# An LSTM's input products: 16 steps of them moved from the head of the sequence to its tail

## The chip, the cores and the metric

The kernel runs on one core of a Trainium2 chip. The metric is the device time of one execution in microseconds (us); three timed runs stand for the kernel before. One further execution was taken by the hardware profiler, and every trace row below is from it.

## The reference

An LSTM over 512 steps with a batch of 32 and 512 hidden units, whose outputs are added to its input. Everything is float32.

```python
xW = einsum('ntd,dg->ntg', x, Wx) + b        # (32, 512, 2048)
def step(carry, xw_t):
    prev_h, prev_c = carry
    a = xw_t + prev_h @ Wh
    i, f, o = (sigmoid(a[:, k*512:(k+1)*512]) for k in range(3))
    g = tanh(a[:, 3*512:])
    next_c = f * prev_c + i * g
    next_h = o * tanh(next_c)
    return (next_h, next_c), next_h
out = x + hs                                  # hs: next_h of all steps
```

`prev_h @ Wh` can only be made step by step (the recurrence). `x @ Wx` (the x products) can be made at any time before its step.

## The kernel before

**The recurrence.** `h_part(t)` multiplies the transposed h by `wh_sb` into two PSUM banks of `gates`: first the columns of i, f and g (384 a quarter), then those of o (128). `cell(t)` follows: sigmoid and tanh on ScalarE (ACT), products and sums on VectorE (DVE), and a transpose `ht` on DVE that releases the next `h_part`. `seed_first` and `seed_last` (ACT) copy the x product of a coming step into its `gates` bank before its recurrence adds to it.

**Three ways to x products.** Steps are grouped in rows of eight (`ROW`).
- *Plain* (`direct`): 16 matmuls of 512 columns a step, straight from the row and `Wx` (`raw`), in four quarters; `keep_direct` adds the bias on DVE. Before the change only steps 0 to 7.
- *Head units* (rows 1 to `HEAD`/8 - 1; four units a row): a fast scheme with seven products in place of eight for two by two blocks of the row and of Wx. It needs differences of Wx (`t_sums`, three DVE instructions for each of the eight pieces of Wx) and of the row (`inner_sums`).
- *Superblocks* of 24 steps (`PER`, three rows): a scheme on top of that with 20 jobs of seven products each (`A_OPS`, `B_OF`, `C_OPS`). Its 14 factors that mix several pieces of Wx are made once by DVE in the head (`make_factors`), written to DRAM (`keep`) and read again for each superblock (`fetch`, into the rings `wa` and `wb`).

Head units and superblocks are drained from PSUM by `evacuate` (ACT and DVE) over five windows; results go by the SP queue to DRAM (`store`), return by `load_xw`, and GpSimd (POOL) adds the bias (`add_bias`).

**The order.** It is written out by hand in windows. Step k has one window, k + 4; steps 0 to 2 have two each (`windows_of`). In a window, after `h_part(k)` is issued, come `evacuate`, DVE's due work (`run_due`), the products of up to five jobs (`products`), `fetch`, `cell(k)` and the seeds. All engines take their instructions in this order. `run_due(v, room)` lets due work in by a price of columns + 160 per instruction up to `room` (`ROOM` = 3400), earlier than due if there is room. Factors are due between window 2 and `START`, the window of the first superblock job, 23 steps (`LEAD`) ahead of its use. The last superblock's jobs therefore end about 20 steps before step 511; those last steps have no x products.

**Start.** `load_raw(q)` loads a quarter of Wx by four transfers of 256 KB. Ten matmuls on zeros run first. Then come the plain products of steps 0 to 3 quarter by quarter, of steps 4 to 7 step by step, then the seeds and the first unit.

Of the kernel before, what the change touches and what calls it, by code (L numbers as in the profile page):

```python
# [9 lines left out]
F32 = mybir.dt.float32  # L10
# [4 lines left out]
P = 128  # L15
B = 32
T = 512
NJ = 4
G = 4
IFG = 3 * P  # L20
ROW = 8
NROWS = T // ROW
C = 256
# [11 lines left out]
R = len(A_OF)  # L35

PER = ROW * MO
HEAD = 7 * ROW
DIRECT = ROW
NSB = (T - HEAD) // PER  # L40
assert HEAD + NSB * PER == T

LEAD = 23
NODES = 8
FIXED = 160
ROOM = 3400
SLACK = [1, 1, 3]
AHEAD = 3
UNITS = [(i, j) for i in range(1, HEAD // ROW) for j in range(NJ)]
# [9 lines left out]
START = windows_of(HEAD - LEAD)[0]  # L59
# [4 lines left out]
def begin(n):  # L64

    return 6 * (n // 5) + n % 5
# [7 lines left out]
def kernel(  # L74
# [9 lines left out]
    nc = tc.nc  # L84
# [19 lines left out]
    bias_sb = const.tile([P, G * P], F32, name="bias_sb")  # L104
    h_init = const.tile([P, NJ, B], F32, name="h_init")
    wh_sb = const.tile([P, NJ, NJ, 2 * C], F32, name="wh_sb")
    raw = [const.tile([P, 4, C], F32, name=f"raw_{i}") for i in range(8)]
    tt_ = [const.tile([P, 4, C], F32, name=f"t_{i}") for i in range(8)]
    single = {b[0][0] for b in B_OF if len(b) == 1}

    rows, xw, stored = {}, {}, {}

    def load_row(i, a=0, b=ROW):
        if i not in rows:
            rows[i] = xpool.tile([P, ROW, NJ, B], F32, name=f"row_{i}", tag="row")
        nc.sync.dma_start(
            out=rows[i][:, a:b].rearrange("p t q b -> p (t q b)"),
            in_=x[i][:, a * P : b * P],
        )
# [10 lines left out]

    def load_raw(q):
        k, e = divmod(q, 2)
        for j in range(NJ):
            nc.sync.dma_start(
                out=raw[NJ * k + j][:, 2 * e : 2 * e + 2].rearrange("p n c -> p (n c)"),
                in_=wx[NJ * k + j][:, 2 * e * C : (2 * e + 2) * C],
            )

    nc.scalar.dma_start(out=bias_t, in_=bias)
    c_init = work.tile([P, P], F32, name="c_init", tag="c", bufs=2)  # L140
# [14 lines left out]
    def t_sums(i):  # L155
        w, t = raw[i], tt_[i]
        return [
            lambda: nc.vector.tensor_sub(t[:, 0:2], w[:, 1::2], w[:, 0:2]),
            lambda: nc.vector.tensor_sub(t[:, 2], w[:, 3], t[:, 0]),
            lambda: nc.vector.tensor_sub(t[:, 3], w[:, 2], t[:, 2]),  # L160
        ]
# [54 lines left out]
    def push_factors():  # L216
        done = []
        ops = [op for n in range(R) if len(B_OF[n]) > 1 for op in make_factors(n)]
        for i, (columns, fn) in enumerate(ops):

            def go(fn=fn):
                fn()
                done.append(fn)

            push(2 + (START - 6) * i // len(ops), columns, go, lambda _, i=i: len(done) == i)
# [28 lines left out]
    def run_due(v, room):  # L254

        i = 0
        while i < len(due):
            window, _, columns, fn, ready = due[i]
            if window > v and (columns + FIXED > room or not ready(v)):
                i += 1  # L260
                continue
            assert ready(window)
            due.pop(i)
            fn()
            room -= columns + FIXED
            i = 0
# [109 lines left out]
    def products(v):  # L376
        for late, ss in ((1, (6,)), (4, (4,)), (2, (7,)), (0, (1,)), (0, (5,)), (1, (5,)), (3, (2, 3))):
            job = jobs.get(v - late)
            for s in ss if job else ():
                if s != 5 or job.w5 == v:  # L380
                    product(job, s)
                if s == 4:
                    job.release()
# [163 lines left out]
    def flat(bank):  # L547
        return bank if len(bank.shape) == 2 else bank.rearrange("p n c -> p (n c)")

    def direct(t, bank, qs=range(4)):  # L550
        i, a = divmod(t, ROW)
        for q in qs:
            k, e = divmod(q, 2)
            for j in range(NJ):
                nc.tensor.matmul(  # L555
                    flat(bank)[j * B : (j + 1) * B],
                    rows[i][:, a, q],
                    raw[NJ * k + j][:, 2 * e : 2 * e + 2].rearrange("p n c -> p (n c)"),
                    start=q == 0,
                    stop=True,  # L560
                    skip_group_check=True,
                )

    def keep_direct(t, bank):
        if t < 4:
            xw[t] = upool.tile([P, G * P], F32, name=f"xw_{t}", tag="xw", bufs=4)
        else:
            xw[t] = node_free[t - 4].rearrange("p t e b -> p (t e b)")
        nc.vector.tensor_add(xw[t], flat(bank), bias_sb)  # L569

    def load_xw(t):
        xw[t] = upool.tile([P, G * P], F32, name=f"xw_{t}", tag="xw", bufs=4)
# [81 lines left out]
    def prepare(v):  # L654

        job = jobs.get(v)
        ops = []
        if job is None or job.w >= START:
            return ops
        i, j = job.kind  # L660
        for k in range(2):
            if (i, k) not in head_sums:
                s, more = inner_sums(block(raw_block(i, k)), f"h{i}{k}")
                head_sums[i, k] = s
                ops += more
            if i == 1:
                ops += t_sums(NJ * k + j)
        job.factors = lambda s: [
            (left(block(raw_block(i, k)), s, head_sums[i, k]), raw_factor(NJ * k + j, s)) for k in range(2)
        ]  # L670
        job.finish = finish_unit(job, i, j)
        job.release = lambda: None
        return ops
# [18 lines left out]
    def fetch(v):  # L692

        job = jobs.get(v + 2)
        if job and job.w >= START and len(B_OF[job.kind[1]]) > 1:
            job.ring = [rpool.tile([P, 3, C], F32, name=f"wa_{job.w}", tag="wa", bufs=3), None]
            nc.sync.dma_start(out=job.ring[0].rearrange("p n c -> p (n c)"), in_=kept[job.kind[1]][0])
        job = jobs.get(v)
        if job and job.w >= START and len(B_OF[job.kind[1]]) > 1:
            job.ring[1] = rpool.tile([P, 4, C], F32, name=f"wb_{job.w}", tag="wb", bufs=4)  # L700
            nc.sync.dma_start(out=job.ring[1].rearrange("p n c -> p (n c)"), in_=kept[job.kind[1]][1])
        sb, rest = divmod(v + 6 - START, PER)
        if v + 6 in UNIT_AT[2 * NJ :: NJ]:
            load_row(3 + UNIT_AT[2 * NJ :: NJ].index(v + 6))
        if rest < MO and 0 <= sb < NSB:
            load_row(HEAD // ROW + MO * sb + (0, 2, 1)[rest])

    with tc.manual_schedule():
        warm = work.tile([P, G, P], F32, name="warm", tag="s")
        nc.scalar.activation(warm[:, 0], c_init, AF.Sigmoid)  # L710
        for m in range(10):
            nc.tensor.matmul(  # L712
                pps[0][0:B].rearrange("p n c -> p (n c)"),
                c_init[:, 0:B],
                c_init.unsqueeze(1).to_broadcast([P, 4, P]),
                start=True,
                stop=True,
            )
        nc.vector.transpose(
            bias_sb.rearrange("p (m l) -> p m l", l=B),  # L720
            bias_t.unsqueeze(2).to_broadcast([P, G * NJ, B]),
        )
        firsts = [gates[0], gates[1], pps[0], pps[1]]
        for q in range(4):
            for t in range(4):
                direct(t, firsts[t], (q,))
        for t in range(4):
            keep_direct(t, firsts[t])
        for t, bank in zip(range(4, ROW), (pps[2], accs[0], accs[1], p5)):
            direct(t, bank)  # L730
            keep_direct(t, bank)
        seed_first(0)
        seed_last(0)
        seed_first(1)
        push_factors()
        for op in prepare(0):
            op()
        products(0)
        for op in prepare(1):
            op()  # L740

        for k in range(T):
            if k % 2 == 0 and k + 2 < T:
                load_residual(k + 2)
            if 2 * 4 - 3 <= k and k + 3 < T:
                load_xw(k + 3)
            h_part(k)
            if 2 * 4 - 2 <= k and k + 2 < T:
                add_bias(k + 2)
            for m, v in enumerate(windows_of(k)):  # L750
                if v == START:
                    assert len(due) == 0 or due[0][0] >= START
                    free.extend(t.rearrange("p (h n) c -> p h (n c)", h=2) for t in others)
                announce(v)
                taken = evacuate(v)
                run_due(v, ROOM - taken)
                products(v)
                fetch(v)
                if k == T - 2:
                    x_last()  # L760
                if m == 0:
                    cell(k)
                    seed_first(k + 2)
                    seed_last(k + 1)
                for op in prepare(v + 1):
                    op()
        assert not due
# [51 lines left out]
```

## Time and profile before

| | |
|---|---|
| median of three runs | 3182.22 us (3182.06 to 3183.36) |
| profiled execution | 3179.14 us |
| its span, first to last instruction | 3177.3 us |
| TensorE (PE) busy | 3120.9 us, 98% |
| VectorE (DVE) busy | 2209.9 us, 70% |
| ScalarE (ACT) busy | 1626.0 us, 51% |
| GpSimd (POOL) busy | 937.8 us, 30% |
| moved by DMA | 639.04 MB, mean 201 GB/s |

PE is TensorE's matmuls, PEld its weight loads. Each float32 matmul appears as two instructions; matmuls into four different 32-row strips of a bank overlap, so spacing tells more than the length of one. In a timeline the square brackets hold the idle time of the engine before the row and what ended it. `p` in the rows is the bank p5, `s_h` a head row's sums, `t` the differences of Wx.

### The profile page before, as it was taken

Reading aid. Unit: us, or ns where it says so; the run is one execution under the profiler, and the core shown is the slowest. Engines: PE = TensorE matmul, PEld = TensorE weight load, DVE = VectorE, ACT = ScalarE, POOL = GpSimd, SP = SyncE. Lnnn points to the kernel's source line nnn. Section 1 sums busy time; section 2 is a strip of 40 time slices with the busy share of each in tenths; the row PEclk is TensorE's granted clock in tenths of the full one; section 3 lists DMA queues with packets and bytes.
Section 4 is the critical chain, followed back from the end, with each engine's and each line's share of the span. In section 5 each row is a group of like instructions: output and inputs, shape, how many; then the busy total and the mean of one; then the engine's idle time right before and its main releaser. Section 6 shows DMA issues by size and latency. Waiting matters only on the chain.

```text
span 3177.3 us, 134411 instructions
## 1 busy us (share of the span) xinstructions
PE 3120.9 (98%) x57012; PEld 2035.9 (64%) x57012; DVE 2209.9 (70%) x6155; ACT 1626.0 (51%) x4890; POOL 937.8 (30%) x1017
## 2 busy tenths in 40 slices
PE   8999999999999999999999999999999999999986
PEld 3666666666666666666666676666766666666653
DVE  4573676767777776767777777767777777767652
ACT  1444555555555555555555555555555555555543
POOL 0122232323232332323232332323232333323232
PEclk9999999999999999999999999999999999999999
DMA  4555576756667666757666576757667576667541
GB/s 170 167 164 159 181 232 195 233 187 224 215 198 228 194 224 203 234 177 235 207 206 229 183 231 207 228 189 242 185 218 224 188 231 199 224 209 230 182 152 61
DMA packets 320857, 639.04 MB, mean 201 GB/s; under 512 B 42880, under 2 KB 108672, under 8 KB 319744
## 3 DMA queue, kind: packets, MB, share of 16 engines
q1 hardware_dynamic: 320112, 630.43, 61.7%
q8 instruction: 449, 7.36, 1.0%
q14 instruction: 152, 1.25, 0.1%
q10 hardware_dynamic: 144, 0.01, 0.0%
HBM read 451.75 MB, written 178.52 MB: 198 GB/s over the span
## 4 chain that ended last, share of the span: by engine, by line
PE 91%; DVE 5%; ACT 2%; DMA 1%; issue 1%; SPq 0%; DVEq 0%
PE gates L596 52%; PE acc L367 16%; PE pp L367 16%; PE p L367 5%; DMA xw<-slot 1%; ACT ig L625 0%; DVE c L624 0%; DVE fc L626 0%; DVE fc L622 0%; DVE ht L631 0%; DVE node L302 0%; ACT pp L406 0%; SPq L424 0%; PE pp L712 0%; PE pp L555 0%
## 5 line engine op out<-in xcount | busy, mean ns | idle before, releaser
L596 PE MATMUL gates<-wh_sb,ht 128*32 128x384 f32 x32704 | 1874.3, 379 | 38.8 <-DVE ht L631 35.5
L596 PEld LDWEIGHTS gates<-wh_sb,ht 128*32 128x32 f32 x32704 | 1131.4, 110 | 794.2 <-issue 659.0
L635 POOL TENSOR_TENSOR oc<-xr,ht 128x128 f32<-128x128 f32 x509 | 300.0, 589 | 2144.5 <-DVE ht L631 2115.3
L577 POOL TENSOR_TENSOR xw<-xw,bias_sb 128x512 f32<-128x512 f32 x504 | 656.1, 1302 | 78.1 <-DMA xw<-slot 35.5
L619 ACT ACTIVATE s<-gates 128x256 f32<-128x256 f32 x512 | 196.8, 384 | 777.7 <-PE gates L596 777.6
L408 DVE TENSOR_TENSOR pp<-acc,p 128x256 f32<-128x256 f32 x404 | 174.6, 432 | 275.5 <-ACT pp L407 261.6
L622 DVE TENSOR_TENSOR fc<-s,c 128x128 f32<-128x128 f32 x511 | 150.1, 294 | 203.9 <-ACT s L619 200.3
L626 DVE TENSOR_TENSOR fc<-s,ig 128x128 f32<-128x128 f32 x512 | 149.6, 292 | 192.7 <-ACT ig L625 192.7
L406 ACT COPY pp<-pu 128x512 f32<-128x512 f32 x404 | 242.1, 599 | 49.0 <-DVE slot L514 18.9
L583 ACT COPY gates<-xw 128x384 f32<-128x384 f32 x508 | 240.3, 473 | 20.9 <-DVE xw L569 20.7
L367 PE MATMUL pp<-wb,node 128*32 128x256 f32 x3040 | 246.1, 379 | 0.0
L621 ACT ACTIVATE s<-gates 128x128 f32<-128x128 f32 x512 | 142.0, 277 | 189.0 <-PE gates L596 188.8
L625 ACT ACTIVATE ig<-c 128x128 f32<-128x128 f32 x512 | 158.7, 310 | 139.1 <-DVE c L624 113.7
L407 ACT COPY pp<-acc 128x256 f32<-128x256 f32 x404 | 145.2, 359 | 139.6 <-DVE slot L514 67.0
L631 DVE STREAM_TRANSPOSE ht<-fc 128x128 f32<-128x128 f32 x511 | 159.1, 311 | 54.6 <-DVE fc L626 0.9
L402 DVE TENSOR_TENSOR pu<-acc,p 128x256 f32<-128x256 f32 x404 | 165.7, 410 | 28.1 <-ACT p L399 27.7
L395 ACT COPY pu<-acc 128x256 f32<-128x256 f32 x404 | 150.3, 372 | 58.5 <-PE acc L367 51.3
L367 PE MATMUL acc<-wb,s 128*32 128x256 f32 x2128 | 172.3, 379 | 0.0
L367 PE MATMUL p<-wa,s 128*32 128x256 f32 x2128 | 172.2, 379 | 0.0
L367 PE MATMUL pp<-wb,s 128*32 128x256 f32 x2128 | 172.1, 379 | 0.0
L367 PE MATMUL acc<-wa,s 128*32 128x256 f32 x2128 | 172.0, 379 | 0.0
L399 ACT COPY p<-p 128x256 f32<-128x256 f32 x404 | 152.7, 378 | 31.0 <-PE p L367 24.6
(130 smaller groups left out, 4049.5 us busy)
## 6 DMA issues: line engine op xcount, KB each, us to landing
wb<-keep_b SPq DMA_DIRECT2D x266, 512.0 KB, 5.6
xw<-xw SPq DMA_DIRECT2D x504, 256.0 KB, 4.1
wa<-keep_a SPq DMA_DIRECT2D x266, 384.0 KB, 4.9
xw<-slot SPq DMA_DIRECT2D x656, 128.0 KB, 3.2
xr<-in_x_dram SPq DMA_DIRECT2D x256, 128.0 KB, 3.1
out_dram<-oc SPq DMA_DIRECT2D x255, 128.0 KB, 2.1
row<-in_x_dram SPq DMA_DIRECT2D x63, 512.0 KB, 6.5
xw<-raw SPq DMA_DIRECT2D x252, 128.0 KB, 3.4
```

Of the source, the lines that this page charges most:

```text
L367: nc.tensor.matmul(dst[t * B : (t + 1) * B], a[:, t], w, start=s in (1, 5) and m == 0, stop=True, skip_group_check=True,)
L399: nc.scalar.copy(job.p5, p5[:, 0])
L402: nc.vector.tensor_add(job.pu[:, 1], job.acc, job.p5)
L406: nc.scalar.copy(job.pp[0], job.pu)
L408: nc.vector.tensor_add(job.pp[1][:, 1], job.acc, job.p5)
L577: nc.gpsimd.tensor_add(xw[t], xw[t], bias_sb)
L583: nc.scalar.copy(gates[t % 2][:, 0:IFG], xw[t][:, 0:IFG])
L596: nc.tensor.matmul(g[j * B : (j + 1) * B, cols], state["ht"][:, k, :], wh_sb[:, k, j, cols], start=False, stop=True, skip_group_check=True,)
L619: nc.scalar.activation(s[:, 0:2], g[:, 0:2], AF.Sigmoid)
L625: nc.scalar.activation(tc_t, c, AF.Tanh)
L631: nc.vector.transpose(ht.rearrange("p q b -> p (q b)"), h)
L635: (nc.gpsimd if t < T - 3 else nc.vector).tensor_add(state["oc"][:, tt % 2], xr[t][:, tt % 2], ht)
```

## The change

- `HEAD` is 40, not 56: the head units make rows 1 to 4 instead of 1 to 6, 16 units instead of 24. `START` is the window of step 17, not 33. There are still 19 superblocks.
- `TAIL`: steps 496 to 511 get plain products. From window `FIRST_TAIL`, the first behind the last evacuation (step 477), every window issues two quarters (`tail_products`), behind `products` and so behind that step's recurrence; the next window adds the bias on DVE (`keep_direct`) and leaves the result in SBUF, so these steps need no `load_xw` and no `add_bias`.
- Two pieces of Wx whose room the superblocks use for sums, and the two last rows, are loaded five windows before.
- `t_sums` of all eight pieces, the row sums of unit 0 and the first factors stand on DVE before and between the bias additions of steps 0 to 7; a new `HEAD_ROOM` of 5000 holds in the head.
- Wx comes in four transfers of 1 MB; six matmuls on zeros, not ten.

```diff
-HEAD = 7 * ROW
-NSB = (T - HEAD) // PER
+HEAD = 5 * ROW
+TAIL = 2 * ROW
+NSB = (T - HEAD - TAIL) // PER
+END = HEAD + NSB * PER
+HEAD_ROOM = 5000
...
-    raw = [const.tile([P, 4, C], F32, name=f"raw_{i}") for i in range(8)]
+    raw_sb = const.tile([P, 8, 4, C], F32, name="raw_sb")
+    raw = [raw_sb[:, i] for i in range(8)]
...
-        for j in range(NJ):
-            nc.sync.dma_start(
-                out=raw[NJ * k + j][:, 2 * e : 2 * e + 2].rearrange("p n c -> p (n c)"),
-                in_=wx[NJ * k + j][:, 2 * e * C : (2 * e + 2) * C],
-            )
+        nc.sync.dma_start(
+            out=raw_sb[:, NJ * k : NJ * k + NJ, 2 * e : 2 * e + 2].rearrange("p j n c -> p j (n c)"),
+            in_=wx[NJ * k : NJ * k + NJ, :, 2 * e * C : (2 * e + 2) * C].rearrange("j p c -> p j c"),
+        )
...
+    FIRST_TAIL = START + PER * (NSB - 1) + begin(R - 1) + 6
+    pieces = [(t, q) for t in range(END, T) for q in range(NJ)]
+    tail_rooms, whole = [], []
+    def tail_bank(t):
+        return (*pps, *accs, p5)[t % 6]
+    def tail_products(v):
...
+        for t in whole:
+            keep_direct(t, tail_bank(t), tail_rooms[t - END])
+        whole.clear()
+        for t, q in pieces[:2]:
+            direct(t, tail_bank(t), (q,))
+            if q == NJ - 1:
+                whole.append(t)
+        del pieces[:2]
...
-            if i == 1:
-                ops += t_sums(NJ * k + j)
...
+        if v == FIRST_TAIL - 5:
+            for i in range(8):
+                if i not in single:
+                    raw[i] = rpool.tile([P, 4, C], F32, name=f"raw_again_{i}", tag="wb", bufs=4)
+                    nc.sync.dma_start(out=raw[i].rearrange("p n c -> p (n c)"), in_=wx[i])
+            for i in range(END // ROW, T // ROW):
+                load_row(i)
...
-        for m in range(10):
+        for m in range(6):
...
+        for i in range(8):
+            for op in t_sums(i):
+                op()
+        for op in prepare(0):
+            op()
+        push_factors()
         for t in range(4):
             keep_direct(t, firsts[t])
         for t, bank in zip(range(4, ROW), (pps[2], accs[0], accs[1], p5)):
             direct(t, bank)
+            run_due(0, 2800)
             keep_direct(t, bank)
         seed_first(0)
         seed_last(0)
         seed_first(1)
-        push_factors()
-        for op in prepare(0):
-            op()
         products(0)
...
-            if 2 * 4 - 3 <= k and k + 3 < T:
+            if 2 * 4 - 3 <= k and k + 3 < END:
                 load_xw(k + 3)
...
-            if 2 * 4 - 2 <= k and k + 2 < T:
+            if 2 * 4 - 2 <= k and k + 2 < END:
                 add_bias(k + 2)
...
-                run_due(v, ROOM - taken)
+                run_due(v, (ROOM if v >= START - 4 else HEAD_ROOM) - taken)
                 products(v)
+                tail_products(v)
```

More of the change, by code (lines that the diff above doesn't have):

```diff
@@ L37 @@
 PER = ROW * MO
-HEAD = 7 * ROW
-DIRECT = ROW
-NSB = (T - HEAD) // PER
-assert HEAD + NSB * PER == T
+HEAD = 5 * ROW
+TAIL = 2 * ROW
+NSB = (T - HEAD - TAIL) // PER
+END = HEAD + NSB * PER
+assert END + TAIL == T
 LEAD = 23
@@ L562, in direct, with keep_direct @@
                 )
-    def keep_direct(t, bank):
-        if t < 4:
+    def keep_direct(t, bank, room=None):
+        if room is not None:
+            xw[t] = room
+        elif t < 4:
             xw[t] = upool.tile([P, G * P], F32, name=f"xw_{t}", tag="xw", bufs=4)
@@ L569, in keep_direct @@
         nc.vector.tensor_add(xw[t], flat(bank), bias_sb)
+    FIRST_TAIL = START + PER * (NSB - 1) + begin(R - 1) + 6
[4 more added lines that the diff above has]
+    def tail_products(v):
+        if v == FIRST_TAIL:
+            tail_rooms.extend(node.rearrange("p t e b -> p (t e b)") for node in node_free)
+            for f in free[: (TAIL - len(tail_rooms) + 1) // 2]:
+                tail_rooms.extend([f[:, 0], f[:, 1]])
+            assert len(tail_rooms) >= TAIL
+        if v < FIRST_TAIL:
+            return
+        for t in whole:
[6 more added lines that the diff above has]
+        del pieces[:2]
     def load_xw(t):
```

## The prediction

> **What bounds the kernel now.** I read the page first, then the chain of waits, then the timeline of TensorE at both ends.
>
> ```profile
> span 3177.3 us, 134411 instructions
> ...
> PE 91%; DVE 5%; ACT 2%; DMA 1%; issue 1%; SPq 0%; DVEq 0%
> ```
>
> TensorE carries 91% of the chain, so time goes away only where TensorE has less to do or stands still less. The profiled execution took 3179.14 us (its span and 1.84 us around it); the three timed runs have a median of 3182.22 us, 3.1 us more. I make the sum against the profiled one and take it off the median. About 0.2% (6 us) is the least change a measurement of this kernel can tell.
>
> The prices come from the chain in order of time (start, length, what, instructions):
>
> ```profile
> 11.45 1.29 PE gates L555 x12
> 12.78 0.39 PE gates L555
> 13.16 1.29 PE pp L555 x12
> ...
> 139.74 3.45 PE gates L596 x64
> 143.19 0.86 PE acc L367 x16
> ```
>
> Sixteen instructions of a plain product (512 columns) are spaced 13.16 - 11.45 = 1.71 us. One recurrence, L596, takes 3.45 us. One of the seven products of a head unit, or two of a superblock product's seven, takes 0.86 us.
>
> ```profile
> 44.19 3.64 PE L596 MATMUL gates<-wh_sb,h_init 128*32 128x384 f32 x64
> ...
> 55.72 1.94 PE L367 MATMUL acc<-t,s_h 128*32 128x256 f32 x16 [2.11 <-DVE pu L402]
> ...
> 71.23 1.07 PE L367 MATMUL acc<-t,s_h 128*32 128x256 f32 x16 [2.50 <-DVE pp L408]
> ...
> 309.08 3.66 PE L596 MATMUL gates<-wh_sb,ht 128*32 128x384 f32 x64
> ...
> 3078.90 3.66 PE L596 MATMUL gates<-wh_sb,ht 128*32 128x384 f32 x64 [1.65 <-DVE ht L631]
> 3084.24 3.66 PE L596 MATMUL gates<-wh_sb,ht 128*32 128x384 f32 x64 [1.68 <-DVE ht L631]
> ```
>
> In TensorE's timeline 44.19 is the recurrence of step 0 and 309.08, counted on, that of step 33, whose window is START. In the last steps nothing is left but the recurrence: one every 5.34 us, bound by the loop through ACT and DVE. Of these TensorE issues for 3.45 us, so 1.89 us are free in each. That is the room the change fills.
>
> **The tail.** NSB stays 19 and START moves from step 33 to step 17, so everything from START to the last superblock product keeps its pattern and comes 16 steps earlier. Behind it stand 16 more bare steps: 16 x 5.34 = +85.4 us. In 32 of them two quarters of a plain product (16 instructions, 1.71 us) stand behind the recurrence in TensorE's queue. 3.45 + 1.71 = 5.16 us, under 5.34: they are hidden by 0.18 us, with nothing but the cell's loop as cover. Without cover they would cost 32 x 1.71 = 55 us. I take 0 and keep +3 us (0.1 us too many in each) for the range; below 0 there is nothing to win, the loop being unchanged. The bias additions run on DVE before the cell needs it, while it waits for the recurrence.
>
> At the seam the SP queue gets four loads of 512 KB (two pieces of Wx, two rows), the Wx pieces waiting for TensorE to let go of a ring buffer. The next load of xw stands behind them.
>
> ```profile
> xw<-xw SPq DMA_DIRECT2D x504, 256.0 KB, 4.1
> ```
>
> It lands 4.1 us after its issue, and needs to be there some 10 us after, before POOL's bias addition and ACT's seed. Two MB in front at 400 GB/s (below) add 5 us and the wait about as much again, so it is about due: I take +1 us, between 0 and +4, once. The factors' writes also move up on SP; the load of xw for step 8 stands behind those of window 8, two steps before its use, which hides it.
>
> **The start.** The DMA view of the first 50 us:
>
> ```profile
> GB/s 0 122 268 248 356 280 326 405 387 400 388 380 383 414 422 413 406 419 426 426 419 398 390 164 25 0 0 0 0 0 0 0 0 0 0 0 13 0 0 0
> ...
> raw<-in_L_cond_Wx_dram SPq DMA_DIRECT2D x16, 256.0 KB, 5.7
> ```
>
> These are slices of 1.25 us. Summed, the first row half and the first quarter of Wx (1.31 MB) have moved by 6.6 us, the second quarter (2.36 MB) by 9.6 and the last (4.46 MB) by 15.0. With some 1.7 us to be reported they land at about 8.3, 11.3 and 16.7 us, if four loads are served in order as the 16 were. Four warm-up matmuls fewer (eight instructions of 512 columns, unpacked 4 x 1.71 / 16 = 0.43 us each) free TensorE 3.4 us sooner, at 8.0 us; plain products start at 8.3 rather than 11.45. But DVE now decides:
>
> ```profile
> 39.00 0.69 DVE L569 TENSOR_TENSOR node<-p,bias_sb 128x512 f32<-128x512 f32 x1 [2.74 <-PE p L555]
> ...
> 46.03 0.68 DVE L158 TENSOR_TENSOR t<-raw 128x512 f32<-128x512 f32 x1
> ...
> 47.56 0.42 DVE L199 TENSOR_TENSOR wa_make<-raw,raw 128x256 f32<-128x256 f32 x1
> ...
> 50.35 0.28 DVE L622 TENSOR_TENSOR fc<-s,c_init 128x128 f32<-128x128 f32 x1
> ...
> 141.73 0.43 DVE L408 TENSOR_TENSOR pp<-acc,p 128x256 f32<-128x256 f32 x1 [4.62 <-ACT pp L407]
> ...
> 144.00 0.28 DVE L622 TENSOR_TENSOR fc<-s,c 128x128 f32<-128x128 f32 x1
> ...
> 145.58 0.31 DVE L631 STREAM_TRANSPOSE ht<-fc 128x128 f32<-128x128 f32 x1
> ```
>
> The differences of one piece of Wx take 47.56 - 46.03 = 1.53 us, a factor of two pieces 50.35 - 47.56 = 2.79 us. In the order of the changed kernel DVE does, from the second quarter's landing: eight differences (11.3 + 12.2 = 23.5), eight row sums (about 1.9 us) and four bias additions (0.7 each), to 28.2; then four times a stretch of factors (2.4, 2.5, 2.7 and 2.7 us by what run_due(0, 2800) lets in) and a bias addition: 41.3 us. TensorE is through its eight steps of plain products at 8.3 + 16 x 1.71 = 35.7 us and waits for the last bank. One product later (0.86 us) step 0 begins at about 42 us, 2.2 us sooner than 44.19. If the loads are late or early this moves by -2 to +4 us.
>
> **The head.** Between step 0 and START the old kernel has 24 x 7 products less 2 done before and 8 done after: 158 x 0.86 + 33 x 3.45 = 249.7 us of TensorE's work in 309.08 - 44.19 = 264.9 us, so 15.2 us idle. The new one has 16 x 7 - 10 = 102 x 0.86 + 17 x 3.45 = 146.4 us of work. Its idle time, by following the queues window by window:
> - Windows 4 and 6 have no recurrence to cover the evacuation, as before (2.50 us at 71.23): 5.0 us, and 0.2 us at window 2. The idle time before step 1 that came from the differences (39 to 55.72) goes.
> - New: in the changed order the factors are through by window 14. In windows 7 to 13 DVE does, after a recurrence starts: the evacuation (141.73 is 2.2 us behind its recurrence), its addition 0.35, factors 3.8 to 4.75 us (room 5000 in the planner's columns, 768 columns at 0.97 us), then the cell, 144.00 to 145.89 = 1.9 us, and 0.13 us to TensorE. That makes 8.55, 8.1, 8.6, 6.5, 7.75, 9.2 and 6.95 us against 7.75, 8.6, 8.6, 6.0, 7.75, 8.6 and 6.0 us of TensorE: 2.8 us over.
>
> Together 8.0 us (5 to 17 with the rival below). START comes at 42.0 + 146.4 + 8.0 = 196.4 us, 112.7 us sooner than 309.08.
>
> **The sum.** -112.7 + 85.4 + 1 = -26.3 us: 3152.8 us on the profiled execution, 3182.2 - 26.3 = 3156 us as the median.
>
> **Rivals.** *The tail's pairs are exposed (slower).* They stand ahead of the next recurrence, and 0.18 us is little.
>
> ```profile
> 46.00:60.00 14.00, 9.77 (x160) 5.12 (x156) 13.11 (x31) 2.73 (x9) 0.81 (x1) 0.88 0.17 67
> ```
> ```profile
> 3130.00:3178.00 48.00, 29.91 (x536) 17.13 (x527) 13.29 (x48) 14.76 (x51) 10.14 (x12) 1.00 0.16 51
> ```
>
> After idle stretches the granted clock (the column before the DMA share) fell, 0.88 in 46 to 60 us, and at 55.72 the sixteen instructions took 1.94 rather than 1.07 us. If the pairs ran at that pace, 3.42 us each, every one of 32 steps would be 1.5 us longer: +49 us, 3205 us. It turns slower from a pair of 2.7 us on (0.18 + 26.3/32 = 1.0 us over). Against it: in the tail the clock is 1.00 with TensorE busy 30 of 48 us, and the pairs make it busier. The Trainium skill (TensorE: Matmul & The Clock Gate, Part 1) has the clock halve after an idle window of about 3.4 us; the trace agrees, since 1.68 us gaps leave the tail at 1.00. 10%.
>
> *DVE bounds the head.* The factors run at loaded durations, beside POOL:
>
> ```profile
> L209 DVE TENSOR_TENSOR wb_make<-wb_make 128x256 f32<-128x256 f32 x10 | 7.4, 743 | 0.0
> ```
> ```profile
> L577 POOL TENSOR_TENSOR xw<-xw,bias_sb 128x512 f32<-128x512 f32 x504 | 656.1, 1302 | 78.1 <-DMA xw<-slot 35.5
> ```
>
> Between 100 and 309 us an L209 (256 columns, like the 0.42 us at 47.56) took 743 ns in the mean. If each of the four windows from 10 on waits out a whole L577 (1.3 us) and the other work is 0.5 us longer in seven, that is +9 us: 3165 us, still faster. The Trainium skill (SBUF — State Buffer, Who interferes with whom) says that a DVE instruction with two SBUF inputs waits for a GpSimd one that holds the shared read port; by that alone, 4 x 1.3 us, it would be 3161 us, and 743 ns agrees that some do. 13%.
>
> *The four loads are served together.* Then no quarter is there before about 16.7 us, DVE's 30 us of work starts there and step 0 comes at 47 us, 5 us later: 3161 us. Against it: 16 loads landed after 5.7 us each, in order. 6%.
>
> *No change:* the tail and DVE each take half, 3%.
>
> **How the numbers follow.** Forecast 68%, DVE 13%, loads 6%: faster 0.87; same 0.03; slower 0.10. The range holds the forecast's own ends (3150, with the loads early, xw in time and DVE quicker; 3163, with the costs at their ends) and reaches to the DVE rival: 3148 to 3167 us.
>
> **What would show it.** Right: step 0 near 42 us; START's recurrence near 196 us; tail steps of 5.34 us with 16 instructions of plain products in each and idle time near 0.2 us. Wrong: tail steps over 5.5 us; recurrences in 87 to 143 us released by DVE with more than 5 us of idle time in all; first plain product after 12 us; a long wait of POOL for xw about 16 steps before the pairs end.

## The result and the profile after

| | before | after |
|---|---|---|
| median, us | 3182.79 (3182.06 to 3184.51, 4 runs) | 3160.38 (3156.52 to 3163.42, 4 runs) |
| profiled execution, us | 3179.14, span 3177.3 | 3159.27, span 3157.5 |

The ratio is 0.9928 [0.9911, 0.9945]: 22.4 us faster on the medians, 19.9 us on the profiled executions. The chain of waits of the changed kernel by engine, from its page:

```profile
PE 85%; DVE 8%; ACT 3%; DMA 2%; issue 1%; SPq 1%; DVEq 0%; POOL 0%; ACTq 0%; POOLq 0%
```

TensorE still carries the chain, but 85% of it instead of 91%. The end is not the reason: from 2964 us on TensorE has 93% of the chain, where it had 51% from 3068 us on before, since the pairs now fill the holes of the cell's loop. Its share fell at the start, where the chain to step 0 now runs through DVE's differences, and in the steady part (83% from 198 to 1000 us, against 94% from 309 to 1109 us before). TensorE's timeline of the changed kernel (start, length, what, and in brackets the idle time before and what ended it):

```profile
7.36 0.63 PE L557 MATMUL gates<-raw_sb,row 128*32 128x512 f32 x3
...
38.28 1.07 PE L369 MATMUL p<-t,s_h 128*32 128x256 f32 x16 [1.57 <-DVE node L573]
39.16 3.64 PE L624 MATMUL gates<-wh_sb,h_init 128*32 128x384 f32 x64
...
59.97 1.93 PE L369 MATMUL acc<-t,s_h 128*32 128x256 f32 x16 [2.50 <-DVE pp L410]
61.68 1.75 PE L369 MATMUL pp<-t,row 128*32 128x256 f32 x16
63.25 1.04 PE L369 MATMUL acc<-t,s_h 128*32 128x256 f32 x16
...
79.75 1.57 PE L369 MATMUL acc<-t,s_h 128*32 128x256 f32 x16 [2.50 <-DVE pp L410]
81.07 1.95 PE L369 MATMUL pp<-t,row 128*32 128x256 f32 x16
82.77 1.46 PE L369 MATMUL acc<-t,s_h 128*32 128x256 f32 x16
84.05 1.05 PE L369 MATMUL acc<-raw_sb,row 128*32 128x256 f32 x16
...
197.87 3.67 PE L624 MATMUL gates<-wh_sb,ht 128*32 128x384 f32 x64
...
2947.58 3.66 PE L624 MATMUL gates<-wh_sb,ht 128*32 128x384 f32 x64
...
2956.89 5.35 PE L624 MATMUL gates<-wh_sb,ht 128*32 128x384 f32 x64 [4.36 <-DVE ht L659]
...
2963.90 3.66 PE L624 MATMUL gates<-wh_sb,ht 128*32 128x384 f32 x64 [1.22 <-DVE ht L659]
2969.20 3.66 PE L624 MATMUL gates<-wh_sb,ht 128*32 128x384 f32 x64 [1.65 <-DVE ht L659]
...
2974.52 3.66 PE L624 MATMUL gates<-wh_sb,ht 128*32 128x384 f32 x64
```

L624 is the recurrence (L596 before), L369 a product of a unit (L367 before), L557 a plain product. Step 0 begins at 39.16, START's step 17 at 197.87, and two steps before the last with units, step 474, at 2947.58. The same two steps in the timeline of before, steps 490 and 492:

```profile
3056.88 3.66 PE L596 MATMUL gates<-wh_sb,ht 128*32 128x384 f32 x64
...
3068.28 3.66 PE L596 MATMUL gates<-wh_sb,ht 128*32 128x384 f32 x64 [1.22 <-DVE ht L631]
```

With the rows of the prediction this divides the span into four stretches:

| stretch, us | before | after | difference | forecast |
|---|---|---|---|---|
| first instruction to START | 309.08 | 197.87 | -111.2 | -112.7 |
| START to step 490 (474) | 2747.8 | 2749.7 | +1.9 | 0 |
| the next two steps, the seam | 11.40 | 16.32 | +4.9 | +1 |
| from step 492 (476) to the end | 109.0 | 193.6 | +84.6 | +85.4 |
| sum | | | -19.8 | -26.3 |

### The profile page after: what moved, and what is told of

Same layout as the page of the kernel before. It is cut to its first block, busy times and chain, and to the rows that moved or that the text cites. A ratio compares the mean times of both kernels' runs of the same rounds, so it can differ in the third digit from the quotient of the medians.

```text
span 3157.5 us, 133431 instructions
## 1 busy us (share of the span) xinstructions
PE 3125.9 (99%) x56620; PEld 2002.8 (63%) x56620; DVE 2198.7 (70%) x6139; ACT 1605.6 (51%) x4842; POOL 915.9 (29%) x1001
## 4 chain that ended last, share of the span: by engine, by line
PE 85%; DVE 8%; ACT 3%; DMA 2%; issue 1%; SPq 1%; DVEq 0%; POOL 0%; ACTq 0%; POOLq 0%
PE gates L624 50%; PE pp L369 15%; PE acc L369 14%; PE p L369 5%; DMA xw<-raw_sb 1%; PE pp L557 1%; DMA xw<-slot 1%; DVE node L304 1%; ACT pp L408 1%; SPq L426 1%; DVE wb_make L201 1%; PE acc L557 1%; DVE c L652 1%; ACT ig L653 1%; DVE fc L654 0%
## 5 line engine op out<-in xcount | busy, mean ns | idle before, releaser
L624 PE MATMUL gates<-wh_sb,ht 128*32 128x384 f32 x32704 | 1873.2, 380 | 20.0 <-DVE ht L659 19.3
L624 PEld LDWEIGHTS gates<-wh_sb,ht 128*32 128x32 f32 x32704 | 1120.8, 110 | 804.6 <-issue 672.6
L605 POOL TENSOR_TENSOR xw<-xw,bias_sb 128x512 f32<-128x512 f32 x488 | 634.1, 1299 | 76.9 <-DMA xw<-xw 36.2
L611 ACT COPY gates<-xw 128x384 f32<-128x384 f32 x492 | 232.7, 473 | 23.0 <-DVE xw L573 21.4
L369 PE MATMUL pp<-wb,node 128*32 128x256 f32 x3040 | 243.6, 379 | 0.0
L369 PE MATMUL acc<-wa,s 128*32 128x256 f32 x2128 | 170.6, 379 | 0.0
L369 PE MATMUL acc<-wb,s 128*32 128x256 f32 x2128 | 170.5, 379 | 0.0
L369 PE MATMUL pp<-wb,s 128*32 128x256 f32 x2128 | 170.5, 379 | 0.0
L369 PE MATMUL p<-wa,s 128*32 128x256 f32 x2128 | 170.5, 379 | 0.0
```

The source lines that it names most:

```text
L369: nc.tensor.matmul(dst[t * B : (t + 1) * B], a[:, t], w, start=s in (1, 5) and m == 0, stop=True, skip_group_check=True,)
L605: nc.gpsimd.tensor_add(xw[t], xw[t], bias_sb)
L611: nc.scalar.copy(gates[t % 2][:, 0:IFG], xw[t][:, 0:IFG])
L624: nc.tensor.matmul(g[j * B : (j + 1) * B, cols], state["ht"][:, k, :], wh_sb[:, k, j, cols], start=False, stop=True, skip_group_check=True,)
```

## The experiments

Diffs are against the changed kernel unless said otherwise. In the order of the argument: the tail, the seam, the start, the head.

**The tail: are the pairs hidden?** Two kernels change only what the tail issues. In the first the odd quarters of its plain products are left out, so that a step has 8 instructions of them; in the second the odd quarters are issued twice, 24 instructions a step.

```diff
         for t, q in pieces[:2]:
-            direct(t, tail_bank(t), (q,))
+            if q % 2 == 0:
+                direct(t, tail_bank(t), (q,))
```

> Leaves out every second quarter of the tail's plain products (the last 16 steps are computed from half of them): 8 instructions stand behind a recurrence in the tail, not 16. If the pairs are hidden by the cell's loop, tail steps stay at 5.31 us and the time at 3160 (within 2 us). If each instruction there costs something, 32 x 0.86 = 27 us at the most go, to 3133.

```diff
             direct(t, tail_bank(t), (q,))
+            if q % 2:
+                direct(t, tail_bank(t), (q,))
```

> Doubles every second quarter of the tail's plain products (the last 16 steps get these twice): 24 instructions stand behind a recurrence, 3.45 + 2.57 = 6.02 us of TensorE's work. If the cover is the 1.86 us up to the next recurrence and no more, each of 32 steps takes 6.02 us rather than 5.31, +0.71 x 32 = +23 us, 3183. If there is more cover than the timeline shows, less; if the pairs were exposed already, 32 x 0.86 = +27 us.

Half took 3160.44 us (ratio 0.9931 [0.9917, 0.9945]), no different from 3160.38. Three quarters in place of two took 3183.05 us (0.9999 [0.9990, 1.0008]), 22.7 us more. TensorE's timeline of the first and then of the second, late in the tail:

```profile
3054.30 3.66 PE L625 MATMUL gates<-wh_sb,ht 128*32 128x384 f32 x64 [0.79 <-ACT gates L616]
3059.61 3.66 PE L625 MATMUL gates<-wh_sb,ht 128*32 128x384 f32 x64 [0.79 <-DVE ht L660]
```
```profile
3056.83 3.66 PE L626 MATMUL gates<-wh_sb,ht 128*32 128x384 f32 x64
3062.86 3.66 PE L626 MATMUL gates<-wh_sb,ht 128*32 128x384 f32 x64
```

With half the products a step lasts 5.31 us, as with all of them, and the brackets show 0.79 us of idle time. With half as many again it lasts 6.03 us, nothing is idle, and TensorE's own work sets the step: 3.45 + 3 x 0.86 = 6.03. The pairs are hidden, and the cover is used up: the next 8 instructions cost 32 x 0.72 = 23 us.

**The seam: what made it late?** SyncE's timeline of the changed kernel at this place (the length is the time that the queue spends on issuing, waits included), and its chain of waits behind it:

```profile
2937.31 3.81 SPq L732 DMA_DIRECT2D raw_again<-in_L_cond_Wx_dram  x2
2941.18 2.35 SPq L119 DMA_DIRECT2D row<-in_x_dram  x2
2943.63 0.38 SPq L602 DMA_DIRECT2D xw<-xw  x1
2944.10 2.64 SPq L426 DMA_DIRECT2D xw<-slot  x4
```
```profile
2946.16 5.98 DMA xw<-slot
...
2952.26 0.70 DVE slot L516
...
2956.89 4.52 PE gates L624 x32
```

Behind the two rows in the SP queue stand a load of xw and the store of a slot (L426, a partial result that leaves so that its buffer can be used again). It is the store that comes late: it takes 5.98 us to land, the DVE instruction that wants the buffer (L516, in `evacuate`) waits for it, and ACT's copy, the cell and the recurrence stand behind that. Two kernels take loads out of this place. The first spreads all four, the second moves the rows alone:

```diff
-        if v == FIRST_TAIL - 5:
+        again = [i for i in range(8) if i not in single]
+        if v in (FIRST_TAIL - 5, FIRST_TAIL - 4):
+            i = again[v - (FIRST_TAIL - 5)]
...
+        if v in (FIRST_TAIL - 16, FIRST_TAIL - 12):
+            load_row(END // ROW + (v - (FIRST_TAIL - 16)) // 4)
```

> Only the four 512 KB loads at the seam are moved: the two last rows 16 and 12 windows before the first tail products, the two pieces of Wx 5 and 4 windows before. If the loads together held up a store on the SP queue, as the changed kernel's trace has it (recurrence of step 475 after 4.36 us of idle time and then at a slow clock), steps 474 to 476 take about 11.4 us as in the old kernel and not 16.3, and the time falls by about 5 us, to 3155. If that hold-up came from the superblock's own stores or by chance, they stay near 16 us and the time stays at 3160.

```diff
         if v == FIRST_TAIL - 5:
...
-            for i in range(END // ROW, T // ROW):
-                load_row(i)
+        if v in (FIRST_TAIL - 16, FIRST_TAIL - 12):
+            load_row(END // ROW + (v - (FIRST_TAIL - 16)) // 4)
```

> The changed kernel with only the two late rows of x loaded earlier (11 and 7 windows sooner); the two pieces of Wx stay together, so the SP queue still stands 3.81 us for the ring buffer. Theory (the rows' 2.35 us of issue and their 1 MB ahead of the slot's store made it late): the store is issued 2.4 us sooner and lands in its usual 3 to 4 us, the two steps of the seam take 11.4 to 12.0 us instead of 16.3, and the time is 3155 to 3156 us, as e1_spread. Rival (the queue's stand for the ring buffer alone made it late): the two steps still take 14 us or more, TensorE idle 3 us or more, 3158 to 3160 us.

Spread, the two steps last 11.41 us, and the time is 3154.53 us (0.9914 [0.9901, 0.9928]). With the rows alone moved, they last 11.41 us as well. Steps 474 to 476 in TensorE's timeline of that kernel, and the slot's stores among its DMA issues around them (size, median us from issue to landing):

```profile
2950.82 3.66 PE L624 MATMUL gates<-wh_sb,ht 128*32 128x384 f32 x64
2956.92 3.66 PE L624 MATMUL gates<-wh_sb,ht 128*32 128x384 f32 x64 [1.14 <-DVE ht L659]
2962.23 3.66 PE L624 MATMUL gates<-wh_sb,ht 128*32 128x384 f32 x64 [1.22 <-DVE ht L659]
```
```profile
xw<-slot SPq DMA_DIRECT2D x4, 128.0 KB, 3.2
```

The store lands in its usual 3.2 us although the SP queue stands as long for the ring buffer as before (3.82 us). So the wait for the ring buffer alone does not cost the seam its 4.9 us: the two rows must be there. Whether they would do it without that wait was not tried. The other traces agree: the same two steps last 13.7 to 17.2 us in all eight kernels that load the rows at this place, and 11.4 us in the four that load them earlier, here and below. The time, 3156.71 us (3152.20 to 3161.60; 0.9916 [0.9902, 0.9929]), scatters too much to show these 4.9 us by itself; the place in the trace does.

**The start and the move, each alone.** The first kernel has the new start but keeps seven head rows and no tail; the second has the old start and the move.

```diff
-HEAD = 5 * ROW
-TAIL = 2 * ROW
+HEAD = 7 * ROW
+TAIL = 0
-HEAD_ROOM = 5000
+HEAD_ROOM = 3400
```

> The old 56 head steps and no plain products in the tail, but the new start (six matmuls on zeros, four loads, early differences and first factors; room 3400). By the changed kernel's trace the new start is worth 5 us at step 0 and some 6 at step 1, less a slow clock after idle stretches: 3171 to 3174. The move of the 16 steps is then worth the other 11 to 14 us, where its cover alone (16 x 1.89 us filled, plain products dearer by 6.6 us) gave 18: the seam's 4.9 us and DVE's 3.3 us in the head are what is missing. If the start is worth 5 us or less, 3177, the move brought all that was forecast.

```diff
-        for m in range(6):
+        for m in range(10):
...
-        for i in range(8):
-            for op in t_sums(i):
-                op()
-        for op in prepare(0):
-            op()
-        push_factors()
...
-            run_due(0, 2800)
...
+        push_factors()
+        for op in prepare(0):
+            op()
```

(The second also has the 16 loads again, and `t_sums` with the first unit's products.)

> The start as before the change (16 loads, ten warm matmuls, differences and first sums behind the bias additions); only the 16 steps are moved from the head to the tail, with a room of 5000 for the factors. Theory (the two parts add up, and e8_start_only leaves 10.7 us of the 22.4 to the move): 3171 to 3173 us, step 0 at 44.2. Rival (the move lives on the new start: with the differences still on DVE's list until step 1, factors crowd into 17 steps and TensorE waits for DVE at steps 1 to 12): 3176 to 3182 us, with over 8 us of waits for DVE between step 0 and START.

The start alone took 3171.08 us (0.9964 [0.9952, 0.9977]; 11.8 us less than before on the same chip), the move alone 3174.34 us (0.9972 [0.9961, 0.9984], 9.2 us less). Together they make 21.0 us, the change 22.4 us: within the spread they add up. The trace of the start alone shows where its gain lies. Step 0 stands at 39.24 us, 5.0 us sooner than before, and START, which is still step 33 here, at

```profile
296.96 3.66 PE L624 MATMUL gates<-wh_sb,ht 128*32 128x384 f32 x64
```

That is 12.1 us sooner than 309.08. Of the 7.2 us that are won between the two, 6.2 lie between step 0 and step 1 (9.5 us instead of 15.7), where TensorE had waited for the differences. At the end of this execution 8.1 us of the 12.1 are left: the steady part is 1.8 us longer, and a hole and a slow recurrence at step 508 cost 2.2.

The second expectation's theory missed its 3173 us by 1.3 us and the rival its 3176 us by 1.7 us, so the time decides between neither. Its trace has 11.8 us of waits for DVE between step 0 and START, which is over the rival's 8; but the changed kernel has 8.3 by the same count, 5.0 of them in the two windows without a recurrence, so only 3.5 us are more. From step 0 to START pass 167.6 us against 158.7. Part of the rest is a slow clock: step 0's recurrence takes 5.81 us up to the next row instead of 3.45, at a granted clock of 0.63 in 44 to 52 us.

**The order of DVE's work.** The differences, the first row sums and the factors go back behind the bias additions; the four loads and six warm-up matmuls stay. (The diff is that of the kernel above without its first two lines.)

> The differences of Wx, the sums of the first unit and the first factors stand behind the bias additions and between the first units again, all else as in the changed kernel. If DVE's early start is what shortened the beginning, step 0 comes near 41 us and step 1 near 57 (39.2 and 48.7 in the changed kernel), and the factors, 11 us of which are no longer done by then, press on more steps of the head: 3168 to 3172. If TensorE's work alone set the head's length, no more than 2 us.

It took 3171.89 us (0.9966 [0.9953, 0.9979]), 11.5 us more than the changed kernel: about all that the new start is worth. TensorE's waits from 36 to 207 us (total, times, longest):

```profile
PE acc L369 <- ACT pu L397: 3.4, 1, 3.4
PE p L369 <- DVE t L160: 3.3, 2, 1.8
PE acc L369 <- DVE pu L404: 2.1, 1, 2.1
```

These 8.8 us, ahead of step 0 and between steps 0 and 1, are what the new order of DVE takes away; one wait of 1.57 us, at 38.28 in the changed kernel, stands in their place.

**The number of loads, and the warm-up.** One kernel has 16 loads of 256 KB again, the other ten warm-up matmuls.

```diff
-            out=raw_sb[:, NJ * k : NJ * k + NJ, 2 * e : 2 * e + 2].rearrange("p j n c -> p j (n c)"),
...
+        for j in range(NJ):
...
+                out=raw[NJ * k + j][:, 2 * e : 2 * e + 2].rearrange("p n c -> p (n c)"),
```

> Wx in 16 loads of 256 KB again, all else as in the changed kernel. If few large loads bring the second quarter sooner, it lands at about 11.5 us here and DVE's first difference starts then, not at 9.4: step 0 some 2 us later, time 3162. If the number of loads does not matter, no change (3160).

```diff
-        for m in range(6):
+        for m in range(10):
```

> Ten matmuls on zeros again, not six, all else as in the changed kernel. TensorE starts its plain products 3.4 us later, at about 10.8 us rather than 7.36. If DVE's queue (differences, row sums, bias additions, first factors) decides when step 0 starts, most of that is absorbed by the 1.57 us wait of TensorE for the last bias addition: step 0 at 40.5 to 41 us rather than 39.2, time 3162. If TensorE decided alone, step 0 at 42.6 and 3164.

With 16 loads it took 3157.24 us (0.9920 [0.9907, 0.9934]); its first plain product stands at 7.47 us and step 0 at 39.01, against 7.36 and 39.16. So step 0 is no later with 16 loads, and my expectation of 2 us fell. But the loads do not land alike. With 16, the second quarter of Wx is whole at 11.2 us, as in the kernel before; with four, at 9.3 us. DVE does not need the whole quarter for its first difference: with 16 loads it waits for one piece of 256 KB, which lands at 9.18 us, with four for all of the quarter. In the kernel with 16 loads:

```profile
9.28 0.69 DVE L161 TENSOR_TENSOR t<-raw_sb 128x512 f32<-128x512 f32 x1 [4.94 <-DMA raw_sb<-in_L_cond_Wx_dram]
```

So it starts at 9.28 us there and at 9.40 in the changed kernel. The first plain product says nothing of the landing: it stands right behind the matmuls on zeros in both. The 3.1 us between the two times lie mostly at the seam, which lasts 13.7 us in this trace and 16.3 in the changed kernel's.

With ten warm-up matmuls the first plain product stands at 10.93 and step 0 at 41.13 us, 2.0 us later, near what was expected if DVE's queue decides. Yet START comes at 198.27, only 0.4 us later, and the time is the same (3160.19 us, 0.9931 [0.9918, 0.9945]). TensorE's timeline of this kernel shows why the 2 us went:

```profile
61.94 1.07 PE L369 MATMUL acc<-t,s_h 128*32 128x256 f32 x16 [2.50 <-DVE pp L410]
68.01 3.64 PE L624 MATMUL gates<-wh_sb,ht 128*32 128x384 f32 x64
```

After the same 2.50 us of idle time the sixteen instructions take 1.07 us here, and 1.93 us at 59.97 in the changed kernel. The next recurrence is 6.07 us away rather than 7.60.

**The room for factors.** First 3400 in the head as elsewhere:

```diff
-HEAD_ROOM = 5000
+HEAD_ROOM = 3400
```

> HEAD_ROOM back to 3400: DVE's factors go over steps 3 to 12 by their due times and not over steps 3 to 9, 3.1 to 6.5 us in a step (by the written order and the trace's durations), with 3.4 to 6.5 us in steps 10 to 12 where the changed kernel has next to none. If DVE bounds these steps, the waits for the transpose come there and grow: START's recurrence 2 to 6 us later than 197.9, time 3162 to 3166. If DVE's room does not matter in the head, no change.

It took 3164.17 us (0.9941 [0.9928, 0.9955]), 3.8 us more. TensorE's waits from step 0 to START, here and then in the changed kernel:

```profile
PE gates L624 <- DVE ht L659: 7.6, 4, 2.2
```
```profile
PE acc L369 <- DVE pp L410: 5.0, 2, 2.5
PE gates L624 <- DVE ht L659: 3.3, 4, 1.1
```

START comes at 204.04 us, 6.2 us later. A smaller room lets fewer factors into the early windows, so more of them crowd later ones: the waits stand at steps 7, 9, 10 and 12 here, at 4, 7, 9 and 10 in the changed kernel. Since the factors can't be had for less, the question is where they lie best. Two kernels spread the seam's loads as above and give more room to windows 2 to 6, where TensorE has most to do, and less from 7 on:

```diff
-run_due(v, (ROOM if v >= START - 4 else HEAD_ROOM) - taken)
+run_due(v, (ROOM if v >= START - 4 else 7000 if 3 <= v <= 6 else 4000 if v > 6 else HEAD_ROOM) - taken)
```

> The seam's loads spread as in e1_spread, and the factors on DVE let in by other rooms: 7000 in windows 3 to 6 (steps 1 and 2 and the evacuations beside them, where TensorE has most to do), 4000 from window 7 on, where 5000 stood. Theory (the 3.3 us that TensorE waited for DVE at steps 4 to 10 come from too large a stretch of factors ahead of the cell): these waits fall under 0.5 us, nothing else is lengthened, START about 3 us sooner relative to step 0 (h0 to START 155.5 us, not 158.7), 3151 to 3152 us against the 3154.5 of e1_spread. Rival (the factors put into windows 3 to 6 hold up the evacuations or the cells of steps 1 and 2 as much): steps 1 to 3 come later by what steps 4 to 10 win, 3154 to 3156 us.

```diff
+run_due(v, (ROOM if v >= START - 4 else 7000 if v in (2, 4, 6) else 5000 if v <= 6 else 3600) - taken)
```

> As e9_rooms, but 7000 only in windows 2, 4 and 6 and 5000 in 1, 3 and 5 (no more than before in windows 3 and 5, which hold a recurrence), 3600 from window 7 on. Theory: waits for DVE at steps 4 to 10 under 0.3 us and steps 1 to 3 no later than in the changed kernel: 3151 us. Rival: windows 4 and 6 have no recurrence to cover DVE, so the larger stretch there comes out as idle time of TensorE before the product units: +1 us in each, 3154 us.

They took 3152.60 us (0.9901 [0.9887, 0.9916]) and 3150.80 us (0.9897 [0.9882, 0.9912]). TensorE's waits from 30 to 215 us in the second:

```profile
PE acc L369 <- DVE pp L410: 5.0, 2, 2.5
PE p L369 <- DVE node L573: 1.5, 1, 1.5
```

No wait for the cell's transpose is left, and from step 0 to START pass 154.7 us (154.1 in the first), not 158.7. The rival of the first came out in part: its two bubbles are 3.1 us each, not 2.5, but what it wins at steps 4 to 10 is more. It also had luck: behind its first bubble TensorE was not slow, which is worth 1.6 us (see the head, below) and which the edit did not aim at. The second is the fastest kernel of this study, about 10 us below the changed one by the medians; 4.1 us of that are the head and 4.9 the seam.

## Why the prediction was right, and where it was off

Forecast 3156 us (3148 to 3167), measured 3160.4: on the profiled executions 6.4 us of the gain are missing. The seam, the head and the steady part took 3.9, 4.3 and 1.9 us more than forecast; the start and the tail gave 2.8 and 0.8 back. So it is in part luck that the first stretch of the table comes within 1.5 us of its forecast.

**The tail held.** 16 x 5.34 = 85.4 us was forecast, 84.6 measured; the steps are 5.31 us, and the rows at 2969.20 and 2974.52 show a pair between two recurrences at that pace. The rival with exposed pairs is out: the granted clock is 1.00 from 2970 to 3140 us, and two kernels with less and more in the pairs show that the margin is small. The prediction worked it out as 0.18 us; with steps of 5.31 us it is 5.31 - 5.16 = 0.15.

**The seam was the right place with the wrong victim and size.** The step that failed: "The next load of xw stands behind them", and +1 us. Measured +4.9. The load of xw was in time (POOL added its bias from 2951.01 us on, 5 us before the transpose that released the recurrence); the store behind the rows was not. I had not asked which other entries of the SP queue stand behind the four loads, and a store is one too, since DVE waits for its buffer. Of the 4.9 us, 3.1 are DVE's wait for it; most of the rest is the recurrence after 4.36 us of idle time, 5.35 us long instead of 3.66.

**The start was sooner by 3 us.** Forecast 42 us for step 0, measured 39.16. DVE's timeline in the changed kernel:

```profile
9.40 0.69 DVE L160 TENSOR_TENSOR t<-raw_sb 128x512 f32<-128x512 f32 x1 [4.95 <-DMA raw_sb<-in_L_cond_Wx_dram]
...
24.64 1.28 DVE L573 TENSOR_TENSOR xw<-pp,bias_sb 128x512 f32<-128x512 f32 x2
...
37.54 0.68 DVE L573 TENSOR_TENSOR node<-p,bias_sb 128x512 f32<-128x512 f32 x1
```

DVE starts on the second quarter at 9.40, not 11.3 us: the landing was the term mis-sized. The prediction read it off the kernel with 16 loads, where the whole second quarter does land at 11.2 us, and took four loads to be served alike. They are not: it lands at 9.25 to 9.52 us in all eleven traces with four loads, and at 11.18 to 11.20 in the three with 16. The bytes move sooner. These are the slices of 1.25 us in the changed kernel, to be held against those of before in the prediction:

```profile
GB/s 0 124 229 403 410 396 387 392 380 388 387 405 420 426 400 419 419 419 419 419 375 415 121 279 357 111 0 0 0 374 351 112 62 397 269 20 60 406 285 340
```

Step 0 is no sooner for it than with 16 loads, as that kernel shows, because DVE's first difference needs only one piece of the quarter; the prediction had the old landing of the whole quarter instead. Its 11.45 for the first plain product of before was a later row of the chain (the timeline has the first at 10.43), which changes nothing, as DVE decides. The working behind it held: 16.5 us to the fourth bias addition (16.9 forecast), 12.3 us to the last (13.1). And as forecast DVE decides, with 1.57 us of waiting at 38.28. That the four loads are served together is out: the quarters land one after another, at 6.6, 9.3, 12.0 and 14.7 us.

**The head was longer by 4.3 us.** 146.4 us of work and 8.0 of idle time were forecast from step 0 to START, and 158.7 us passed. The idle time was nearly right: the brackets show 5.0 us in the two windows without a recurrence, and 3.3 us for DVE, at steps 4, 7, 9 and 10, where 2.8 us stood in the working. So "DVE bounds the head" is out at the rival's size of 9 us more, although its mechanism is there, and the kernels with other rooms take it away. What the step left out is TensorE's slow stretch after each bubble: from 59.97 to 63.25 two groups are spaced 3.28 us instead of 2 x 0.86, from 79.75 to 84.05 three are spaced 4.30 instead of 2.58, together 3.3 us. The windows of the changed kernel show the granted clock (the column before the DMA share):

```profile
60.00:80.00 20.00, 17.50 (x295) 9.25 (x298) 9.76 (x24) 6.70 (x18) 0.46 (x1) 0.92 0.49 152
80.00:100.00 20.00, 19.34 (x329) 11.02 (x325) 11.76 (x27) 6.78 (x19) 0.46 (x1) 0.91 0.33 105
...
160.00:200.00 40.00, 40.00 (x736) 26.77 (x731) 9.95 (x33) 18.29 (x53) 8.49 (x10) 1.00 0.57 170
```

I had priced the bubbles as idle time alone, by the one of before at 71.23 (1.07 us behind it), though the row at 55.72 in the prediction showed 1.94 us after 2.11 us of idle time. The second bubble of before, of the same kind, was slow as well (from 89.47 the next three groups are spaced 4.30 us instead of 2.58):

```profile
89.47 1.78 PE L367 MATMUL acc<-t,s_h 128*32 128x256 f32 x16 [2.49 <-DVE pp L408]
```

The rest of the head can be placed too. A bracket counts from the recorded end of the row before it, which lies 0.2 us behind the spacing that the prices go by (1.07 against 0.86); counted by spacing the six holes are 9.5 us, not 8.3. And the work was one product less than forecast: nine of the head's products stand behind START now, not eight as before, so 101 x 0.863 + 17 x 3.453 = 145.9 us. With 9.5 and 3.3 that makes 158.7.

**The steady part** took 1.9 us more, forecast as nothing. TensorE's waits in it, in the changed kernel and then before:

```profile
PE gates L624 <- DVE ht L659: 5.5, 18, 1.1
```
```profile
PE gates L596 <- DVE ht L631: 2.2, 10, 0.4
```

They are 3.3 us more, and the ninth product behind START is 0.9 us. The same stretch lasts 2748.6 to 2753.6 us in the traces of the twelve kernels above, all of them longer than the one trace of before. So a small cost of the change is likely, but which part of it costs this no run here tells.

## What to carry to other kernels

When loads are put into a queue, list everything queued behind them, stores as well: a store whose buffer is to be used again is as much on the path as a load. Price a hole in TensorE's work as the hole and the slow stretch that may follow it. Landings read from small loads do not hold for large ones, and what a first consumer waits for is the load that brings its piece. A bare loop has a sharp margin: what fits is free, and the next instruction costs its whole length in every step.

## What the runs showed of the hardware

*The clock falls after short holes, but not always.* With a room of 3400 in the head, TensorE's timeline has three lengths of hole in one execution:

```profile
119.73 5.23 PE L624 MATMUL gates<-wh_sb,ht 128*32 128x384 f32 x64 [2.25 <-DVE ht L659]
...
139.69 3.66 PE L624 MATMUL gates<-wh_sb,ht 128*32 128x384 f32 x64 [1.77 <-DVE ht L659]
...
166.10 5.35 PE L624 MATMUL gates<-wh_sb,ht 128*32 128x384 f32 x64 [2.17 <-DVE ht L659]
```

After 2.17 and 2.25 us the recurrence took 5.2 to 5.4 us, at a granted clock of 0.68 and 0.69; after 1.77 us it took 3.66, at 1.00. With the start alone a hole of 2.03 us, at 3143.74, was enough (5.34 us, clock 0.68). But after 2.50 us (ten warm-up matmuls, 61.94) nothing was slow, and with the move alone not even after 3.40 us at its seam; both at a clock of 1.00. The Trainium skill (TensorE: Matmul & The Clock Gate, Part 1) has the clock halve after an idle window of about 3.4 us that runs freely, without regard to when the kernel starts. That the same hole costs or not as all before it shifts by 2 us agrees with a free-running window; that 2.0 to 2.3 us are enough does not agree with a whole window of idle time.

*Four loads of 1 MB brought the second quarter of Wx 1.9 us sooner than sixteen of 256 KB:* whole at 9.3 us against 11.2, and the last quarter at 14.7 against 16.6 to 16.8. Why the small ones move their bytes more slowly at first was not tried.
